# A masked scan over the first tokens of layer 0, with the full scan behind a branch on the chip

## The chip, the cores and the metric

One core of one Trainium2 chip. The metric is the device time of one execution in microseconds (us), as the median of repeated executions. Where two kernels are compared, a ratio is given: the mean time of one kernel's runs over the mean time of the other's runs of the same rounds. It is therefore not quite the ratio of the two medians that are quoted.

The engines in the profile: PE is the matrix engine, PEld its weight loads, DVE the vector engine, ACT the scalar engine, POOL the GpSimd engine, SP the engine that here only issues transfers.

## The reference, cut to what matters

Two layers run one after the other on one picture of 64 x 64 tokens with 96 channels. Each has a group norm, a projection to 192 channels, a 3x3 depthwise convolution, four directional scans with 16 states, a layer norm with a gate, a projection back and a residual add. Layer 1 uses an ordinary recurrence. Layer 0 writes its scan as a quotient and a product:

```python
dt = softplus(dt @ dt_proj_w + dt_proj_b)
A = -exp(A_log)                                     # -1 .. -16 here
log_dA = einsum('bld,dn->bldn', dt, A)
dB_u = einsum('bld,bln->bldn', dt, B_mat) * u[..., None]
decay = exp(cumsum(log_dA, axis=1))                 # over all tokens, never reset
h = decay * cumsum(dB_u / (decay + 1e-12), axis=1)
y = einsum('bldn,bln->bld', h, C_mat) + u * D_skip
```

The decay is the exponential of a sum that only falls. With dt near 0.693, state 1 reaches exp(-110.9) after 160 tokens, and that is exactly 0 in fp32. From there on h is 0 times a finite number, so those tokens add nothing. State n gets there n times sooner. Of 4096 tokens and 16 states, only a small corner has any effect, and the change uses this.

## The kernel before: the parts that the change and the argument touch

The scans work on tiles of 128 rows, 1024 tokens at a time, for two pairs of opposite directions, three tiles and 16 states: 384 iterations in each layer. The parts under `l == 0` are what the change does away with.

```python
def load_exp_ln():
    """Exp, Ln and the copies from one activation table: no reload between them."""
    tc.keep_in_program_order(nc.scalar.preload_act_table_set("natural_log_exp_and_others"))
...
def stage_a(j):                       # one of 384 iterations
    b_ps = broadcast("B", j)          # PE: a selecting product, 2 x 512 columns
    nc.scalar.activation(dec, state[k]["dt"][T], AF.Exp, scale=am[:, T, n : n + 1])
    nc.vector.tensor_mul(b, b_ps, du)
    if l == 0:
        nc.scalar.activation(inv, dec, AF.Ln, bias=eps12)      # 1 / (decay + 1e-12)
        nc.scalar.activation(inv, inv, AF.Exp, scale=-1.0)
        nc.gpsimd.tensor_mul(b, b, inv)
def stage_s(j):
    nc.vector.tensor_tensor_scan(s, dec if l else ones, b, carry..., ALU.mult, ALU.add)
    c_ps = broadcast("C", j)
    if l == 0:
        nc.vector.tensor_mul(dec, c_ps, dec)
        nc.vector.tensor_mul(dec, s, dec)
def stage_r(j):                       # the sum over the states, in PSUM
    nc.tensor.matmul(ps[:, cut], ident, v[:, cut], start=(n == 0), stop=(n == NS - 1))
...
# the close: layer norm, gate, out_proj, residual
for g in range(8):
    nc.tensor.matmul(ps, ipw_s[:, c0 : c0 + m], xn, ...)       # z, fp32, 512 columns
    nc.scalar.activation(sz[b][...], ps, AF.Silu)
load_exp_ln()
for g in range(8):
    nc.tensor.matmul(pc[0], cen, y0[:, cut], start=True, stop=False)   # y minus its mean
    ...
```

## Time and profile before

| | us |
|---|---|
| median of 3 runs | 5496.6 (5489.5 to 5501.2) |
| span of the profiled run | 5493.0 |
| front of layer 0, to the last convolution result | 180.9 |
| scans of layer 0 | 2745.9 |
| gap | 0.2 |
| close of layer 0, to layer 1's first statistics | 136.6 |
| layer 1 | 2429.4 |

The borders of the stages are read from the order of time. The front ends where the last convolution result is copied out, the scans end with the last add into y, and the close starts with PE's next product. Here are only three rows of the costliest groups. Each row gives line, engine, operation, operands and shapes, then how many, then the busy time, the mean of one in ns, and the idle time ahead of them:

```profile
L421 POOL TENSOR_TENSOR b<-b,inv 128x1024 f32<-128x1024 f32 x384 | 1276.9, 3325 | 805.4 <-ACT inv L420 608.5
...
L430 DVE TENSOR_TENSOR_SCAN s<-ones,carry,b 128x1024 f32<-128x1024 f32 x288 | 739.3, 2567 | 1.1 <-POOL b L421 1.1
L430 DVE TENSOR_TENSOR_SCAN s<-dec,carry,b 128x1024 f32<-128x1024 f32 x288 | 688.9, 2420 | 0.0
```

The rows with `ones` are layer 0's scans, those with `dec` are layer 1's. POOL's product with the inverse of the decay is layer 0's alone.

### The profile page before, as it was taken

Reading aid. Unit: us, or ns where it says so; the run is one execution under the profiler, and the core shown is the slowest. Engines: PE = TensorE matmul, PEld = TensorE weight load, DVE = VectorE, ACT = ScalarE, POOL = GpSimd, SP = SyncE. Lnnn points to the kernel's source line nnn. Section 1 sums busy time; section 2 is a strip of 40 time slices with the busy share of each in tenths; the row PEclk is TensorE's granted clock in tenths of the full one; section 3 lists DMA queues with packets and bytes.
Section 4 is the critical chain, followed back from the end, with each engine's and each line's share of the span. In section 5 each row is a group of like instructions: output and inputs, shape, how many; then the busy total and the mean of one; then the engine's idle time right before and its main releaser. Section 6 shows DMA issues by size and latency. Waiting matters only on the chain.

```text
span 5493.0 us, 25105 instructions
## 1 busy us (share of the span) xinstructions
PE 3867.1 (70%) x7592; PEld 1346.8 (25%) x7592; DVE 4677.4 (85%) x3360; ACT 2195.4 (40%) x2729; POOL 2288.8 (42%) x1014
## 2 busy tenths in 40 slices
PE   8766666666666666666677987767676777676678
PEld 2222222222222222222221222222222222222223
DVE  4499999999999999999994429999999999999951
ACT  2355555454454555555553223223232233232221
POOL 0576767666467676676661033123222223121000
PEclk9778778686677777877887568888888888888875
DMA  0000000000000000000000000000000000000000
GB/s 21 0 0 0 0 0 2 0 1 0 0 0 0 0 0 0 0 3 1 0 0 0 0 0 0 0 0 0 0 0 0 0 0 0 0 0 0 0 2 10
DMA packets 11063, 6.67 MB, mean 1 GB/s; under 512 B 10176, under 2 KB 10416, under 8 KB 10928
## 3 DMA queue, kind: packets, MB, share of 16 engines
q1 hardware_dynamic: 8816, 4.30, 0.3%
q8 instruction: 59, 0.97, 0.1%
q10 hardware_dynamic: 2112, 0.79, 0.1%
q14 instruction: 76, 0.62, 0.0%
HBM read 3.51 MB, written 1.57 MB: 1 GB/s over the span
## 4 chain that ended last, share of the span: by engine, by line
DVE 36%; PE 27%; issue 24%; POOL 10%; ACT 2%; DMA 0%; POOLq 0%; DVEq 0%; SPq 0%; ACTq 0%
DVE s L430 17%; PE y L460 11%; DVE b L415 8%; PE cv L251 4%; DVE hc L447 3%; POOL ln L372 3%; DVE dec L443 3%; PE bc_C L401 2%; PE bc_B L401 2%; POOL t L371 2%; DVE dec L442 2%; POOL b L421 1%; POOL du L375 1%; PE in L222 1%; POOL rl L374 1%
## 5 line engine op out<-in xcount | busy, mean ns | idle before, releaser
L421 POOL TENSOR_TENSOR b<-b,inv 128x1024 f32<-128x1024 f32 x384 | 1276.9, 3325 | 805.4 <-ACT inv L420 608.5
L401 PE MATMUL bc_C<-C,sel 96*128 96x512 bf16 x1536 | 553.8, 448 | 1045.0 <-DVE dec L442 536.1
L460 PE MATMUL y<-dec,ident 128*128 128x512 f32 x1536 | 1103.7, 858 | 245.0 <-DVE dec L443 208.1
L413 ACT ACTIVATE dec<-dt,am 128x1024 f32<-128x1024 f32 x768 | 879.7, 1146 | 864.5 <-PE y L460 561.3
L415 DVE TENSOR_TENSOR b<-bc_B,du 128x1024 f32<-128x1024 f32 x768 | 934.3, 1217 | 84.8 <-PE bc_B L401 83.6
L460 PE MATMUL y<-hc,ident 128*128 128x512 f32 x1536 | 921.1, 732 | 21.7 <-DVE uy L473 11.4
L401 PEld LDWEIGHTS <-sel 96*128 96x128 bf16 x3072 | 329.0, 108 | 2175.9 <-issue 2092.4
L430 DVE TENSOR_TENSOR_SCAN s<-ones,carry,b 128x1024 f32<-128x1024 f32 x288 | 739.3, 2567 | 1.1 <-POOL b L421 1.1
L430 DVE TENSOR_TENSOR_SCAN s<-dec,carry,b 128x1024 f32<-128x1024 f32 x288 | 688.9, 2420 | 0.0
L401 PE MATMUL bc_B<-B,sel 96*128 96x512 bf16 x1536 | 529.5, 430 | 124.3 <-DVE b L415 118.3
L439 ACT COPY carry<-s 128x1 f32<-128x1 f32 x576 | 108.4, 188 | 1213.0 <-DVE s L430 1212.4
L460 PEld LDWEIGHTS y<-dec,ident 128*128 128x128 f32 x1536 | 368.7, 264 | 811.2 <-issue 391.2
L443 DVE TENSOR_TENSOR dec<-s,dec 128x1024 f32<-128x1024 f32 x384 | 539.7, 1406 | 0.2
L371 POOL TENSOR_TENSOR t<-w,t 128x512 f32<-128x512 f32 x96 | 138.0, 1438 | 856.1 <-DVE t L370 855.9
L447 DVE TENSOR_TENSOR hc<-bc_C,s 128x1024 f32<-128x1024 f32 x384 | 464.7, 1210 | 1.7 <-PE bc_C L401 1.7
L442 DVE TENSOR_TENSOR dec<-bc_C,dec 128x1024 f32<-128x1024 f32 x384 | 460.9, 1200 | 0.0
L419 ACT ACTIVATE inv<-dec,eps 128x1024 f32<-128x1024 f32 x384 | 440.7, 1148 | 28.0
L460 PEld LDWEIGHTS y<-hc,ident 128*128 128x128 f32 x1536 | 359.4, 236 | 369.7 <-issue 300.9
L420 ACT ACTIVATE inv<-inv 128x1024 f32<-128x1024 f32 x384 | 405.8, 1057 | 11.8
L372 POOL TENSOR_TENSOR ln<-ln,t 128x512 f32<-128x512 f32 x96 | 259.3, 2701 | 7.4
L251 PE MATMUL cv<-pad,diag 64*64 64x512 f32 x288 | 246.3, 1056 | 0.0
L430 DVE TENSOR_TENSOR_SCAN s<-ones,b 128x1024 f32<-128x1024 f32 x96 | 230.2, 2398 | 4.5 <-POOL b L421 4.5
(123 smaller groups left out, 2936.7 us busy)
## 6 DMA issues: line engine op xcount, KB each, us to landing
out_dram<-ob SPq DMA_DIRECT2D x8, 192.0 KB, 2.2
xw<-in_xpw_dram SPq DMA_DIRECT2D x4, 306.0 KB, 2.8
xt<-in_x_dram ACTq DMA_DIRECT2D x4, 192.0 KB, 4.4
xt<-in_x_dram SPq DMA_DIRECT2D x4, 192.0 KB, 3.2
ipw<-in_ipw_dram SPq DMA_DIRECT2D x2, 144.0 KB, 4.3
ab<-in_alb_dram SPq DMA_DIRECT2D x4, 25.5 KB, 3.2
op<-in_opw_dram SPq DMA_DIRECT2D x2, 48.0 KB
dw<-in_dtw_dram SPq DMA_DIRECT2D x4, 18.0 KB
```

The costliest lines, as they stand in the source:

```text
L251: nc.tensor.matmul(ps.rearrange("p (h w) -> p h w", w=HW), diag[:, k, :], pad1[:, r + i : r + i + 8, j : j + HW], start=(k == 0), stop=(k ...
L372: nc.gpsimd.tensor_add(ln, ln, t)
L401: nc.tensor.matmul(ps[:, cut], selector(T, n), state[k][which][:, cut], start=True, stop=True)
L413: nc.scalar.activation(dec, state[k]["dt"][T], AF.Exp, scale=am[:, T, n : n + 1])
L415: nc.vector.tensor_mul(b, b_ps, du)
L419: nc.scalar.activation(inv, dec, AF.Ln, bias=eps12)
L421: nc.gpsimd.tensor_mul(b, b, inv)
L430: nc.vector.tensor_tensor_scan(s, dec if l else ones, b, carry[T][:, n : n + 1] if c else 0.0, ALU.mult, ALU.add,)
L442: nc.vector.tensor_mul(dec, c_ps, dec)
L443: nc.vector.tensor_mul(dec, s, dec)
L447: nc.vector.tensor_mul(hc, c_ps, s)
L460: nc.tensor.matmul(ps[:, cut], ident, v[:, cut], start=(n == 0), stop=(n == NS - 1))
```

## The change: its intent, and the diff

Layer 0 scans 160 tokens for state 1, 80 for state 2, 56 for states 3 and 4, 32 for 5 to 8 and 20 for 9 to 16, for four directions. All are laid end to end in one row of 2560 columns. One masked scan serves many pieces: `state = mask * state + b`, with a mask of 0 at the first token of each piece. The chip then checks that every dropped piece has a decay of exactly 0 (exponent below -105), and only otherwise runs the full scan.

The full scan computed 2 x 3 x 16 x 4096 = 393,216 columns of up to 128 rows. The short one computes 2 x 2560 = 5120 columns, 77 times fewer.

The diff, cut to its core. Comments were also stripped, so the line numbers of the two kernels differ, and the body of the full scan moved into a function unchanged:

```diff
+CUT = ((0, 1, 160), (1, 2, 80), (2, 4, 56), (4, 8, 32), (8, 16, 20))
+GONE = 105.0
 ...
+    def first_tokens(l, pw):
 ...
+            sel4 = po.tile([32, 32, 128], F32, name="sel4")
+            nc.gpsimd.tensor_copy(
+                sel4, ident[0:32, 0:32].unsqueeze(2).to_broadcast([32, 32, 128])
+            )
+            xs = po.tile([128, 2, XS], F32, name="xs")
+            nc.gpsimd.memset(xs, 0.0)
 ...            # six copies of weights into xs; mask memsets; ud = first tokens of u
+            for a, b in ends(u0, ud[0]):
+                nc.vector.tensor_copy(b, a)
 ...            # projection, softplus (Abs, Exp, Ln), running sum s of dt
+                for n0, n1, ln, off in GROUPS:
+                    for n in range(n0, n1):
+                        nc.scalar.activation(de[...], s[:, :, 0:ln], AF.Exp,
+                            scale=am[0:m, T, n : n + 1])
+                    nc.scalar.activation(wi[:, cut], de[:, cut], AF.Ln, bias=eps12[0:m])
+                    nc.scalar.activation(wi[:, cut], wi[:, cut], AF.Exp, scale=-1.0)
+                    nc.gpsimd.tensor_mul(q, q, dt[...])
 ...
+            for ci, (off, wd, parts) in enumerate(CHUNKS):     # 7 chunks
 ...                # PE: B and C of each piece to all rows, by fp32 selecting products
+                for b, m in enumerate((128, 64)):
+                    nc.vector.tensor_mul(bb[:, 0:wd], bp[0:m, 0:wd], w[b][:, cut])
+                    nc.vector.tensor_tensor_scan(
+                        st[:, 0:wd], mask[0:m, cut], bb[:, 0:wd], 0.0, ALU.mult, ALU.add)
+                    nc.vector.tensor_mul(cd[:, 0:wd], cp[0:m, 0:wd], dec[b][:, cut])
+                    nc.vector.tensor_mul(cd[:, 0:wd], cd[:, 0:wd], st[:, 0:wd])
 ...                # PE: the sum over the states, one fp32 product for each state and half
 ...
+            return nc.values_load(flag[0:1, 0:1], min_val=0, max_val=1, ...)
 ...
-        # ---- the four scans ----
 ...
+        if l == 0:
+            bad = first_tokens(l, pw)
+            with tc.If(bad > 0):
+                for g in range(4):
 ...                # y set back to u * D
+                all_tokens(l, pw)
+        else:
+            all_tokens(l, pw)
```

## The prediction

> **What bounds the kernel now.** I read the busy shares by slice first, then a table of stretches, then the order of time at each border, then the groups by shape.
>
> The page's slices (each is 137 us; a digit is tenths busy):
>
> ```profile
> PE   8766666666666666666677987767676777676678
> DVE  4499999999999999999994429999999999999951
> POOL 0576767666467676676661033123222223121000
> ```
>
> DVE shows two plateaus of 9, with a dip between them: the scans of layer 0 and of layer 1. In both, the vector engine sets the pace; POOL is heavy in the first only (it multiplies by 1/decay). The table of stretches (us; busy time and count of PE, weight loads, DVE, ACT, POOL; granted clock) says the same in numbers, one stretch of each kind:
>
> ```profile
> 57.00:181.00 124.00, 123.83 (x145) 32.52 (x144) 26.66 (x23) 20.77 (x25) 0.00 (x0) 1.00 0.00 0
> 1000.00:2000.00 1000.00, 659.52 (x1211) 216.41 (x1209) 955.43 (x626) 526.28 (x577) 632.55 (x239) 0.74 0.00 0
> 3104.00:3228.00 124.00, 123.23 (x146) 31.90 (x145) 25.96 (x23) 21.47 (x26) 0.70 (x1) 0.50 0.00 0
> 3500.00:4500.00 1000.00, 702.98 (x1651) 276.47 (x1651) 930.57 (x649) 295.73 (x438) 238.54 (x155) 0.85 0.00 0
> ```
>
> The convolutions are all PE (124 of 124 us), the scans 93 to 96% DVE. The borders come from the timeline: the last convolution result of layer 0 is copied out at 180.87, layer 0's closing stage starts at 2926.96, and layer 1's statistics at 3063.55:
>
> ```profile
> 180.87 0.68 ACT L259 ACTIVATE uy<-cv,v 64x512 f32<-64x512 f32 x1 [13.93 <-PE cv L251]
> 2926.96 3.94 PE L509 MATMUL z<-xn,ipw 96*128 96x512 f32 x4 [4.82 <-DVE uy L473]
> 3063.55 4.25 DVE L181 BATCH_NORM_STATS2 st<-xT 96x6 f32<-96x512 f32 x7
> ```
>
> So the span of 5493 us is: front of layer 0 181, **scans of layer 0 2746**, its close 137, all of layer 1 2429. Nothing of layer 1 can start early: it reads the finished residual stream.
>
> [...]a load starts at 183.23 and the next copy at 184.52, 1.29 us later. I use 1.28. [...] The trace has both paces: one half of an fp32 product over 512 columns is issued every 0.854 us in the convolution, every 0.427 us in the projections at 187 us. But the profile's own clock column says 1.00 for that slow convolution and 0.50 for layer 1's equally slow one, so I go by durations.
>
> **The change, part by part.**
>
> *Removed:* the stretch from 180.9 to 2927.0, 2746 us, provided the branch skips the full scan. The flag is set only where some channel's sum A*dt over the kept tokens is above -105. Evaluating the reference's own formulas on its inputs, dt lies between 0.6929 and 0.6935 and the weakest of these sums is -110.9; the branch skips.
>
> *Added:* the short scan. Its width is 640+320+448+512+640 = 2560 elements for each of two channel blocks, in 7 chunks. What each engine has to do, with durations by shape from before:
>
> - ACT: the new code lets Exp and Ln alternate without pinning the shared table; the built program's order has 25 table loads between the first token copy and the flag: 25 x 1.283 = 32 us. An activation costs 0.20 us + 0.84 ns per element (629 ns at 512, 1057 at 1024): per block 26 of them over 7680 elements, 11.6 us, two blocks 23; softplus 12 x 0.47 = 6; small copies 5. Sum 66 us, nearly serial.
> - DVE: a multiply is 692 ns at 512 and 1217 at 1024 (0.17 us + 1.03 ns per element), the scan 1.23 and 2.35 us (0.11 + 2.19). A chunk of N in one block is three multiplies and a scan, 0.62 us + 5.28 ns x N: 14 x 0.62 + 5120 x 5.28 ns = 36 us; softplus, cumsum and adds some 17 more.
> - PE: short fp32 products pay their weight load. The closest thing before is layer 1's output product, 96 columns each:
>
> ```profile
> 5400.94 0.74 PE L554 MATMUL o<-op,g 64*128 64x96 f32 x2
> 5401.61 0.50 PEld L555 LDWEIGHTS o<-ident,xT 96*128 96x128 f32 x2 [0.17 <-issue]
> 5401.61 0.74 PE L555 MATMUL o<-ident,xT 96*128 96x96 f32 x2
> 5401.99 0.55 PEld L553 LDWEIGHTS o<-op,g 128*128 128x128 f32 x2
> ```
>
> Three such products repeat every 1.77 us, 0.59 each. The last four chunks have 28 selecting and 56 summing products; half of the latter have 64x64 weights (0.28 us a pair of loads, not 0.50), so about 0.45 each: 84 x 0.45 = 38 us, more than DVE's 22 us for those chunks.
>
> The path in time, from 181: POOL makes the selectors once the convolution's memory is free (4096 elements at 1.04 us per 1024, memsets, six copies) to 188.5; four projection products at the slow pace and their copies to 194; three softplus halves of 4.0 us on ACT (0.47 x 3 + two table loads) to 206; block 0's decays and weights, 10 loads and 13 us of activations, to 232; DVE's cumsum for block 1, 235; first weights of block 1, 242. Only then can the chunks run in their order, block 1 being in each: 33 us of DVE work remain (275), but PE finishes its short products nearer 254 + 38 = 291; I take 286. Copies out of PSUM and twelve adds: 292. **So the new stage is 111 us.** [...]
>
> *Moved:* everything after the branch waits for it. The built order shows layer 0's close now interleaved differently: 10 table loads where there were 2 (Silu between Exp and Ln work), and layer 1's decay constants wait on the scalar queue for weights whose transfers are now issued only after the branch (two of 306 KB, 2.8 us to landing, and four small ones). PE held that stretch (36.0 of 37 us busy), with single PSUM buffers, so ACT's delays show: 8 x 1.28, some under PE's work, plus a few us of DMA: 12 us. Layer 1's matmul order is the same as before, so its 2429 us stay.
>
> Sum: 2746 removed, 111 + 5 + 12 = 128 added, net 2618. 5496.6 - 2618 = 2879; I say **2880**.
>
> **The rivals.** *The branch is taken on the chip:* both scans, about 5620 us. The margin of 5.9 in an exponent and dt's spread of 0.0006 speak against it; 2%. [...] *PE runs warm in the short stage:* its products halve, DVE ends it at 275 to 278, and the time is 2868. For: projections at 187 us ran at 0.427. [...] *The jump stalls:* skipping thousands of instructions on every engine costs tens of us; 2900 to 2920. Nothing before measures it. *Layer 1 changes pace:* its multiplies waited 80 us for broadcasts of PE, so a better or worse granted clock could move it by some 1%; within one trace the clock is steady over each plateau, with no slow drift, which speaks against.
>
> **Range and chances.** Layer 0's front and layer 1 are 2610 us measured and hardly touched; the short stage may be 90 to 150 us, the branch 2 to 25, the close 137 to 165. Unlisted waits between engines add, rarely subtract, so the range leans up: 2840 to 2940. Faster by over 2%: 0.975; within 2%: 0.005; slower: 0.02.
>
> **What would show each step.** Chunk, decay and table-load rows between 181 and about 292, with 25 loads of 1.28 us; no full-scan row of layer 0 at all; PE, not DVE, last in the chunk stage; the gap at the branch under 10 us on every engine; a close of about 149 us; a layer 1 of 2429 us. Wrong would be: a stage far longer than 111 us because hops between engines outweigh the work, or a layer 1 that runs at another pace.

## The result, and the profile after

The changed kernel takes **2870.2 us** (median of 4 runs, 2867.0 to 2875.5) against 5496.5 us for the kernel before (4 runs, 5489.5 to 5501.2). The ratio is 0.522 (0.5215 to 0.523). It gives the right result.

The slices of the page, each now 72 us:

```profile
PE   7966888987676676776676777667767666667888
...
DVE  7125227028999999899999999999999899999221
ACT  1235412133222323232332223233232322222210
POOL 0012000047220322322032223103221301000000
```

Of DVE's two plateaus of 9, only one is left. The short scan lies in the third and fourth slice (143 to 286 us), where DVE has 2 and 5 and ACT 3 and 5: no engine is near full. Of the groups of before, no row of layer 0's full scan is left. Layer 1's row is:

```profile
L336 DVE TENSOR_TENSOR_SCAN s<-dec,carry,b 128x1024 f32<-128x1024 f32 x288 | 688.6, 2419 | 0.0
```

2419 ns against 2420: layer 1 is as it was. The table of stretches of the changed kernel, for the convolution, the short scan and the close (us; busy time and count of PE, weight loads, DVE, ACT, POOL; granted clock, DMA share, GB/s):

```profile
57.00:181.00 124.00, 123.79 (x145) 31.95 (x144) 26.68 (x24) 20.82 (x25) 0.04 (x1) 1.00 0.00 0
180.80:290.70 109.90, 61.73 (x213) 42.08 (x213) 57.62 (x112) 66.86 (x103) 24.24 (x26) 1.00 0.00 1
294.60:438.80 144.20, 124.22 (x157) 27.53 (x158) 36.33 (x66) 41.34 (x59) 0.00 (x0) 0.73 0.01 3
```

The second row is the new stage: in 109.9 us no engine is busy for more than 67. It is a chain through several engines, not the work of one. The granted clock in these rows is no guide: the repeat of this kernel (the first experiment) shows 0.50 for the same convolution, busy for 124.00 of 124 us, where this trace shows 1.00. So PE's pace is read from durations. (The trace lists an fp32 product as two records, its halves: the eight summing products over 128x64 elements are 16 records. The counts of PE are records.) By stage:

| us | before | after |
|---|---|---|
| front of layer 0 | 180.9 | 180.8 |
| scans of layer 0 | 2745.9 | 109.9 |
| gap (branch) | 0.2 | 3.9 |
| close of layer 0 | 136.6 | 144.2 |
| layer 1 | 2429.4 | 2426.3 |
| span | 5493.0 | 2865.1 |

So 2636.0 us went, 3.7 came with the branch, 7.6 with the close, and layer 1 gave 3.1.

Inside the short scan the waits of 181 to 295 us tell the order (who waited for whom: us in total, times, longest):

```profile
POOL fw L521 <- ACT fw L519: 33.5, 8, 5.9
ACT fyt L595 <- PE fy L583: 28.9, 2, 28.6
...
DVE fcd L575 <- PE fy L583: 13.1, 8, 3.4
```

First POOL waits for ACT's weights. Then ACT has long been done and waits for PE's summing products (28.6 us in one piece), and DVE waits for PE too (13.1 us in eight waits), because its buffers come free only when PE has read them. The stretch of the last chunks alone, 247.5 to 288.1 us, shows who holds it:

```profile
247.50:288.10 40.60, 40.58 (x181) 34.51 (x180) 26.03 (x48) 11.54 (x21) 5.08 (x3) 1.00 0.01 1
```

PE is busy for 40.58 of 40.60 us.

The border at the branch, in order of time (start, duration, engine, what, and the idle time before it with its end):

```profile
288.63 2.11 DVE L597 TENSOR_TENSOR uy<-uy,fyt 64x160 f32<-64x160 f32 x6
...
291.31 1.28 ACT L752 ACT_TABLE_LOAD   x1 [2.67 <-ACTq L728]
...
294.61 2.05 PE L761 MATMUL c<-y,cen 128*128 128x512 f32 x2 [6.53 <-DVEq L728]
294.73 1.00 DVE L659 TENSOR_SCALAR xn<-xT,gst 96x512 f32<-96x512 f32 x2 [3.98 <-DVEq L728]
```

DVE ends its last add at 290.74 and does nothing until 294.73. PE waits for DVE's sequencer. That is the gap. What the sequencers do in it is seen by line: L599 loads the flag into a register, L728 is the branch. First the flag's load of DVE, then DVE's and PE's events at the branch (duration in ns as least/median/most, then the start in us):

```profile
L599 DVEq TENSOR_LOAD <-flag x1: 544/544/544, 290.7 to 290.7; - x1
```

```profile
L728 PEldq COMPARE_BRANCH  x1: 3512/3512/3512, 286.8 to 286.8; - x1
...
L728 DVEq COMPARE_BRANCH  x1: 72/72/72, 291.3 to 291.3; - x1
L728 DVEq EVENT_SEMAPHORE  x1: 21/21/21, 294.4 to 294.4; - x1
```

DVE's flag is loaded in 0.54 us and compared in 0.07 us by 291.3, but the next event on DVE is at 294.4. Those 3.1 us lie after the comparison and ahead of the first instruction at the jump's target.

### The profile page after: what moved, and what is told of

It is laid out like the page before. It is cut to its first block, busy times and chain, and to the rows that moved or that the text cites. A ratio compares the mean times of both kernels' runs of the same rounds, so it can differ in the third digit from the quotient of the medians.

```text
span 2865.1 us, 13371 instructions
## 1 busy us (share of the span) xinstructions
PE 2125.8 (74%) x4445; PEld 793.2 (28%) x4445; DVE 2143.1 (75%) x1728; ACT 807.5 (28%) x1189; POOL 498.7 (17%) x356
## 4 chain that ended last, share of the span: by engine, by line
PE 40%; issue 24%; DVE 18%; POOL 5%; ACT 1%; POOLq 0%; DVEq 0%
PE y L366 16%; DVE hc L353 7%; DVE s L336 6%; PE cv L714 4%; PE bc_C L307 4%; PE bc_B L307 3%; DVE b L321 3%; PE z L751 2%; POOL t L277 2%; PE v L771 2%; POOL ln L278 1%; PE in L685 1%; PE c L762 1%; PE c L761 1%; PE c L763 1%
## 5 line engine op out<-in xcount | busy, mean ns | idle before, releaser
L336 DVE TENSOR_TENSOR_SCAN s<-dec,carry,b 128x1024 f32<-128x1024 f32 x288 | 688.6, 2419 | 0.0
L307 PE MATMUL bc_C<-C,sel 96*128 96x512 bf16 x768 | 272.8, 442 | 507.3 <-DVE hc L353 505.9
L321 DVE TENSOR_TENSOR b<-bc_B,du 128x1024 f32<-128x1024 f32 x384 | 467.2, 1217 | 76.4 <-PE bc_B L307 75.5
L319 ACT ACTIVATE dec<-dt,am 128x1024 f32<-128x1024 f32 x384 | 439.1, 1145 | 298.4 <-DVE s L336 297.0
L307 PEld LDWEIGHTS <-sel 96*128 96x128 bf16 x1536 | 159.5, 105 | 959.1 <-issue 907.9
L307 PE MATMUL bc_B<-B,sel 96*128 96x512 bf16 x768 | 247.4, 405 | 3.9 <-DVE b L321 3.2
L336 DVE TENSOR_TENSOR_SCAN s<-dec,b 128x1024 f32<-128x1024 f32 x96 | 227.3, 2394 | 0.0
L278 POOL TENSOR_TENSOR ln<-ln,t 128x512 f32<-128x512 f32 x48 | 114.8, 2391 | 3.8
L714 PEld LDWEIGHTS cv<-pad,diag 64*64 64x64 f32 x288 | 63.9, 223 | 182.2 <-issue 182.2
L230 PE MATMUL pj<-uc,xw 128*96 128x512 f32 (+1 forms) x160 | 88.2, 666 | 23.1 <-DVE rl L271 20.7
L280 POOL TENSOR_TENSOR dt<-ln,rl 128x512 f32<-128x512 f32 x48 | 101.8, 2120 | 3.8
```

What stands on the lines that cost most here:

```text
L230: nc.tensor.matmul(ps[0:m], xw[:, T, c0 : c0 + m], uc[T][:, h * 512 : (h + 1) * 512], start=(T == 0), stop=(T == 2),)
L278: nc.gpsimd.tensor_add(ln, ln, t)
L280: nc.gpsimd.tensor_add(dt, ln, r)
L307: nc.tensor.matmul(ps[:, cut], selector(T, n), state[k][which][:, cut], start=True, stop=True)
L714: nc.tensor.matmul(ps.rearrange("p (h w) -> p h w", w=HW), diag[:, k, :], pad1[:, r + i : r + i + 8, j : j + HW], start=(k == 0), stop=(k ...
```

## The experiments

The theory at the outset had five parts. In the first half of the short stage, ACT's table loads set the pace. In its second half, PE's short fp32 products do. At the branch, DVE's jump over the full scan costs some 4 us. POOL's first work delays the start. In the close, ACT's added table loads cost some 10 us. Its rivals: DVE is the bound of the chunks, the comparison itself (and the flag's load) is what costs at the branch, or the close varies by itself and ACT has nothing to do with it.

The experiments ran in three groups: the first two on one chip, the last (the branch taken, the second early-decay run and the third run of the changed kernel) on another. A first run repeated the changed kernel, as their base.

> The changed kernel once more, as the yardstick of this group: about 2870 us (2866 to 2876), with 110 us from the last convolution result (181) to the last add into y (291), a gap of 4 us at the branch, a close of 144 us and a layer 1 of 2426 us.

Measured: 2877.8 us (2876.2 to 2879.3, 5 runs), ratio 0.523. The profiled run has a short stage of 109.8 us and a close of 148.4 us. The stage is the same to 0.1 us, while the close is 4 us longer. The close of a kernel that did not change already varies, so in the experiments stages are compared by their own borders.

### Tables pinned in the short scan

```diff
+            load_exp_ln()
             sel4 = po.tile([32, 32, 128], F32, name="sel4")
```

> One table that holds Exp and Ln is loaded ahead of the short scan, so 25 loads become 1. My theory (ACT sets the pace until block 1's first weights are there, at 242): 19 of the 25 loads lie before that moment, 19 x 1.283 = 24 us come off, the stage falls from 110 to about 86 us and the time to about 2846 us. Rival 1 (the chunk work of DVE and PE sets the pace throughout): under 5 us. [...]

Measured: 2852.1 us (2825.0 to 2861.2), ratio 0.518 (0.5159 to 0.5203). The stage falls from 109.9 to 92.1 us. ACT's busy time in it falls from 66.9 to 34.4 us, so the loads are gone; 25 x 1.283 = 32.1 us is what they took. Only 17.8 us come off the stage. In the table of stretches, the first row is the whole stage, the second its part from the end of the wait for weights:

```profile
180.40:272.50 92.10, 62.41 (x214) 42.06 (x213) 62.02 (x110) 34.43 (x79) 23.34 (x26) 0.50 0.00 1
...
220.20:270.50 50.30, 48.14 (x193) 37.61 (x192) 35.14 (x62) 9.41 (x25) 6.45 (x5) 0.50 0.00 1
```

From 220 us on PE is busy for 48.1 of 50.3 us, and ACT waits 40.5 us for it in one piece. In the changed kernel this stretch of PE began at 238.5 us and ended at 288.1, so it was as long, and the whole gain lies ahead of it. There stood 19 of the 25 loads, 24.4 us; the other six, 7.7 us, lay beside PE's work and were worth nothing. The loads were the pace of the first half, as the theory said, but its size (24 us, a stage of 86) was not reached: some 18 of the 24.4 us came off, mostly because ACT now waits 5.9 us for DVE ahead of that stretch, against 1.3 before. Rival 1 (under 5 us) is false.

### The sum over the states with bf16 operands

```diff
-                    nc.vector.tensor_mul(cd[:, 0:wd], cd[:, 0:wd], st[:, 0:wd])
+                    cb = wk.tile([m, 512], BF16, tag="cb", name=f"fcb{b}{ci}")
+                    nc.vector.tensor_mul(cb[:, 0:wd], cd[:, 0:wd], st[:, 0:wd])
 ...
-                                    ident[0:m, 0:m],
+                                    idb[0:m, 0:m],        # the identity in bf16
```

The summed terms are rounded to bf16. The outputs are right.

> The products that sum over the states take bfloat16 operands, one pass of TensorE in place of two [...]; DVE's and ACT's instructions stay the same in number and size. Theory (from about 247 on PE's short products, not DVE, set the pace): some 112 half products of the last four chunks become 56, about 10 us less PE work, of which DVE takes back a little: the stage ends 7 to 10 us sooner, 2861 us. Rival (DVE sets the pace of the chunks): under 2 us.

Measured: 2859.7 us (2856.9 to 2865.0), ratio 0.520 (0.5196 to 0.5211). The stage falls to 95.9 us, by 14.0. The stretch of the last chunks in the table:

```profile
247.50:274.00 26.50, 20.27 (x117) 17.01 (x117) 26.40 (x46) 11.59 (x22) 4.44 (x3) 1.00 0.00 2
```

Now DVE is busy for 26.40 of 26.50 us and PE for 20.3. The trace lists one pass in place of two: the summing products over 128x64 elements are 16 records in the changed kernel and 8 here. The theory had the direction, but not the size: PE's work fell by 20.3 us, not by 10, and the stage by 14.0, not by 7 to 10. This is the cleanest reversal: the same chunks, DVE's work unchanged (26.0 us before, 26.4 now), and the bound moved from PE to DVE. The rival "DVE is the bound" is false for the changed kernel. It holds only once PE has been relieved, and 14 us is all that PE held beyond DVE.

### POOL's first work in another order

```diff
-            sel4 = po.tile([32, 32, 128], F32, name="sel4")
-            nc.gpsimd.tensor_copy(sel4, ...)
             xs = po.tile([128, 2, XS], F32, name="xs")
 ...        # xs and mask
+            sel4 = po.tile([32, 32, 128], F32, name="sel4")
+            nc.gpsimd.tensor_copy(sel4, ...)
```

> GpSimd makes the small projection operand first and the selectors (3.66 us) last. Theory (the first projection waits for GpSimd's queue, 6.9 us of PE idle put down to it): projections start 4 to 5 us sooner, the stage is 105 us and the time about 2866 us. Rival (DVE's six token copies, which took 6.7 us beside GpSimd's copy, hold the projection just as long): under 1.5 us.

Measured: 2867.7 us (2839.7 to 2875.1), ratio 0.521 (0.5186 to 0.5229). The time does not separate from the base; the stage does, at 106.2 us, 3.7 less (4 to 5 were expected). The start of the stage in the changed kernel:

```profile
180.93 6.67 DVE L452 COPY ud<-u 128x160 f32<-128x160 f32 x6 [97.17 <-PE cv L714]
180.96 3.66 POOL L414 COPY sel<-ident 32x4096 f32<-32x4096 f32 x1 [156.74 <-PE cv L714]
...
187.73 1.39 PE L460 MATMUL xd<-ud,xs 128*102 128x320 f32 x2 [6.94 <-POOL xs L421]
```

And with the order changed:

```profile
181.14 3.29 DVE L452 COPY ud<-u 128x160 f32<-128x160 f32 x6 [97.17 <-PE cv L714]
...
184.24 1.39 PE L460 MATMUL xd<-ud,xs 128*102 128x320 f32 x2 [3.23 <-POOL xs L417]
```

PE starts 3.7 us sooner after the end of the convolution (it idles 3.23 us, not 6.94). There is a second reading: DVE's six copies took 6.67 us beside POOL's large copy and take 3.29 us without it. In the changed kernel one of the two copies of 128x160 elements took 3.79 us beside POOL's copy of 3.66 us (they ended at 184.7 and 184.6 us), and the other, after them, took 0.38 us. But the copies are not what held PE. In the new order PE starts at 184.24 us, before the last copy ends (184.43), so its first product does not need all six. The two that it needs, of the first two directions, are these copies of 128x160, and in the changed kernel they were done at 185.0 us, 2.7 us before PE began. So POOL's queue was the last wait, as the theory had it.

### Layer 1's decay constants made at the start

In the changed kernel these constants are made after the branch, and their Exp pulls table loads into the close (ten there, of 1.28 us each, against two in this version). This version makes them at the very start:

```diff
+    def decays(l):
 ...        # the load of ab, am = -exp(ab), each with a buffer of its own
+    dec_l = [decays(0), decays(1)]
     for l in range(2):
 ...
-            ab = wts.tile([128, 3, NS + 1], F32, tag="ab", name=f"ab{lp}")
-            nc.sync.dma_start(out=ab, in_=alb[lp])
-            am = wts.tile([128, 3, NS], F32, tag="am", name=f"am{lp}")
-            nc.scalar.activation(am, ab[:, :, 0:NS], AF.Exp)
-            nc.vector.tensor_scalar_mul(am, am, -1.0)
+            ab, am = dec_l[l][p]
```

> Layer 1's decay constants are loaded and made at the very start, so that no Exp of theirs stands among the Silus after the branch; 10 table loads after the branch become 2. Theory (ACT delays PE in the close): the close falls from 144 to about 137 us, as in the kernel before, and the time by 7 us to 2863 us. Rival (PE's slow pace hides it): under 2 us.

Measured: 2854.1 us, ratio 0.5205 (0.5189 to 0.5221). The six runs fall into two groups: 2851.8 to 2855.8 (four) and 2873.8 to 2874.4 (two). The profiled run is of the quick group, with a close of 126.0 us. That looks like 18 to 22 us gained. But the very same kernel was run again later:

> The early-decay variant once more, in the same group as the changed kernel. Same pace on both sides: 0 to 4 us less than the changed kernel (the table loads and the late decay constants cost almost nothing by themselves, since TensorE idled 20 us in the close with 10 loads and with 2). If fewer loads make the quick pace likelier: mostly 2852 here against mostly 2870 beside it.

Measured: 2870.5 us, ratio 0.521 (0.5191 to 0.5228), again in two groups: 2848.6 and 2852.1, and 2870.5 to 2875.4 (three). This time the profiled run is of the slow group. The stretch of the close in the first run:

```profile
295.10:421.10 126.00, 106.05 (x157) 24.52 (x158) 36.24 (x64) 30.83 (x49) 0.00 (x0) 0.78 0.00 0
```

And in the second run of the same kernel:

```profile
294.30:438.80 144.50, 125.05 (x157) 27.49 (x158) 36.24 (x64) 30.81 (x49) 0.00 (x0) 0.67 0.00 2
```

157 records of PE in both, and 30.8 us of ACT in both, without the added loads. PE needs 106 us for them once and 125 us the other time, and it is idle 19.9 and 19.5 us. A row of the groups by shape shows where, in the first run:

```profile
L759 PE MATMUL z<-xn,ipw 96*128 96x512 f32 x16 | 9.8, 697 | 0.0
```

And in the second:

```profile
L759 PE MATMUL z<-xn,ipw 96*128 96x512 f32 x16 | 16.4, 1130 | 0.0
```

The same 16 instructions take 697 ns on average in one run and 1130 ns in the other. The whole difference lies in these first products: all of `z` is done by 316 us in the first run and by 331 us in the second, and the later groups of the close repeat every 13.7 to 13.8 us in both. The close's length is set by PE's pace in that run, and that pace is not of the program alone. The granted clock of the rows (0.78 and 0.67) moves the same way.

### A second branch close by

```diff
                 all_tokens(l, pw)
+            with tc.If(bad > 0):
+                nc.scalar.mul(y0[:, 0:1024], u0[:, 0:1024], ds[:, 0:1])
```

> A second branch on the same flag right behind the first, over one scalar instruction, no second read of the flag. Theory (most of the 4 us is the long jump with a new fetch of instructions, and the meeting of the engines): the second gap is under 1.5 us, 2871 us. Rival (every branch costs the same): a second gap of about 4 us, 2874 us.

Measured: 2857.1 us (2856.1 to 2870.2), ratio 0.5205 (0.5194 to 0.5216), nominally faster by half a per cent although it does more. Its stage is 109.8 us and its gap 4.0 us, against 109.9 and 3.9. A second comparison and a short jump cost about 0.1 us. DVE's events show it: the second comparison takes 56 ns, and the wait of 3.2 us lies between the first comparison (291.3) and its target (294.6), as in the changed kernel:

```profile
L734 DVEq COMPARE_BRANCH  x1: 56/56/56, 294.7 to 294.7; - x1
```

So the gap is not the comparison. What made this version faster is again the close, at 129.3 us:

```profile
294.80:424.10 129.30, 107.95 (x157) 25.45 (x158) 36.33 (x65) 42.17 (x60) 0.00 (x0) 0.76 0.01 3
```

This close has all ten table loads and the same order of ACT's instructions as the changed kernel's, and ACT is even busier (42.2 us against 41.3). It is 15 us shorter, because PE took 108 instead of 124 us. This is the second witness against the theory that ACT's loads make the close long.

### No branch and no fallback

```diff
-            return nc.values_load(flag[0:1, 0:1], ...)
+            return None
 ...
-            bad = first_tokens(l, pw)
-            with tc.If(bad > 0):
-                ...
+            first_tokens(l, pw)
```

It is right for these inputs only: on others, nothing would catch a decay that has not vanished.

> No flag is read, no branch, no fallback (right on these inputs, not safe on others). Theory (the branch costs its own gap and the close has nothing that could have been moved ahead of it): 4 us less, 2866 us. Rival (the branch is a wall to the scheduler): the z products of the close, 31 us of PE, move into the short scan, where PE is idle for most of the first 57 us, and the time falls by 15 to 30 us, to 2840 to 2855 us.

Measured: 2844.8 us (2843.3 to 2850.3), ratio 0.518 (0.5172 to 0.5186), all five runs in the quick group. At the border:

```profile
287.81 1.46 DVE L597 TENSOR_TENSOR y<-y,fyt 128x160 f32<-128x160 f32 x6 [1.22 <-ACT fyt L595]
...
289.37 2.07 PE L750 MATMUL c<-y,cen 128*128 128x512 f32 x2 [0.62 <-ACT fyt L595]
```

PE starts the close's first product 2.1 us before the last add into y has ended. In the changed kernel it starts 3.9 us after that. So the branch costs 3.9 + 2.1 = 6.0 us directly. The rest of the 25 us between the medians is the close, 124.1 us here at the quick pace. The time lies in the rival's range (2840 to 2855 us), but by luck: the close's gate products did not move into the short scan, and the first `z` product starts at 293 us, after the first `c` products. For other work the branch was a wall: without it layer 1's decay constants are made in the short scan (DVE changes a sign for them at 286.2 us), and the close has two table loads, not ten.

### The branch taken

```diff
-GONE = 105.0
+GONE = 1000.0
```

> The threshold is raised to 1000, which no sum reaches, so the flag is set and the full scan runs behind the short one. Theory: the kernel before's 2746 us of layer 0's scans come back on top of everything: 2870 + 2746 + about 8 us for setting y again = 5620 to 5630 us, correct. Rival (the full scan inside the branch is scheduled worse): over 5660 us.

Measured: 5618.8 us (5616.1 and 5621.5), ratio 1.0227. Short scan and full scan run one after the other, as the rival of the prediction had it. The border again:

```profile
288.50 2.04 PE L230 MATMUL pj<-u,xw 128*108 128x512 f32 x2
...
289.37 1.15 ACT L731 ACTIVATE y<-u,ds 128x1024 f32<-128x1024 f32 x1 [0.24 <-DVE y L597]
```

Here nobody jumps over anything. PE goes on without a listed wait, ACT starts 0.24 us after the add that it needs, and POOL starts 0.8 us after DVE's last add (291.25 to 292.01), once DVE has its flag. Flag, load and comparison are the same as in the changed kernel. So of the 4.0 us that DVE stands still there, at most 0.8 is the flag and the comparison, and the other 3.1 to 3.2 us are the **jump over the full scan**. What happens in it the DMA view tells: between 286 and 296 us the changed kernel's trace has six transfers of instructions (8 or 16 KB each). PE, ACT and DVE make their comparisons in this stretch, at 286.8, 288.8 and 291.3 us. Two more lie between 258 and 263 us, around POOL's comparison at 258.9, and only three in the other 101 us from 180 to 286. So the jumps go with a fetch of instructions; how the 3.1 us divide within it is not shown. PE pays for its own jump too (its comparison is on record with 3.5 us, from 286.8 on), but that lies beside work that PE had already been given, and PE waits for DVE in any case.

### The changed kernel a third time, and the parts together

> The changed kernel again, now beside the early-decay variant on one chip. So far its nine timed runs in two groups were all 2867 to 2879 us, while a variant with the same closing code gave 2856 three times of four in another group. If the chip or the session sets TensorE's pace in layer 0's close, most runs here are either all near 2855 or all near 2874, like the variant's beside it. If the code sets it, this kernel stays at 2867 to 2879 and the variant at 2852.

Measured: 2868.8 us (2865.9 to 2877.9), ratio 0.522 (0.5214 to 0.5229). Stage 109.8, gap 4.2, close 148.1, layer 1 2433.6 us. Three profiled runs of the changed kernel have stages within 0.1 us of each other, closes of 144.2, 148.4 and 148.1 us and layers 1 of 2426.3, 2433.6 and 2433.6 us. None of its 14 timed runs is of the quick group.

The last version joins the pinned tables, the bf16 sum, POOL's order and the early decay constants, with branch and fallback kept.

> Pinned table, early decay constants, bfloat16 sums and GpSimd's new order together. If the four gains add: 24 + 7 + 8 + 4.5 = 43 us less, 2827 us, with a stage of about 73 us and a close of 137 us. If the gains lie behind one another (DVE's chunk work of 36 us and softplus take over): 2835 to 2845 us.

Measured: **2818.2 us** (2814.3 to 2841.0), ratio 0.5145 (0.5126 to 0.5165): faster than both kernels, and 2.1% under the 2877.8 us of the changed kernel on the same chip. Part of this is pace: the profiled run has the quick close, 126.1 us. The two slow runs, 2840.5 and 2841.0, are 37 us under the changed kernel, which is what the stage gives. The stage is 72.5 us, 37.4 less:

```profile
180.30:252.80 72.50, 39.82 (x150) 24.62 (x149) 57.66 (x111) 34.34 (x79) 23.52 (x26) 0.50 0.00 1
```

DVE has the largest share now, 57.7 of 72.5 us. Of the four parts three touch this stage; alone they gave 17.8, 14.0 and 3.7 us, 35.5 as a sum, and together they give 37.4. Why the sum is exceeded was not looked into. Its five runs again split: 2814.3 to 2818.2 (three), and 2840.5 to 2841.0 (two).

## Why the prediction was right, point by point

The time, 2870 us, is 10 us under the predicted 2880 and inside the range.

- **What is removed.** Predicted 2746 us. No row of the full scan of layer 0 is left, and the branch skips. Shown, and the taken branch shows the other side: 5619 us, as the rival said (about 5620).
- **The short scan.** Predicted 111 us, measured 109.9, and 109.8 in two repeats. Its steps hold too. There are 25 table loads of 1.28 us. The second block's first weights were predicted for 242 us; POOL starts on them at 241.9 and DVE uses them at 243.5. PE, not DVE, is last: the bf16 version shows it directly. PE's last four chunks were sized at 38 us, and its busy stretch at the end is 40.6.
- **The branch.** The sum of the prediction has 5 us for it, with no trace behind it; the gap is 3.9 to 4.2. The records of the sequencers, the second branch and the taken branch divide the 4.0 us of DVE: 0.6 for flag and comparison, 3.1 for the jump, the rest around them. That instructions are fetched there is seen in the six transfers.
- **Layer 1.** Predicted unchanged at 2429 us; the three runs of the changed kernel show 2426 to 2434.
- **The close: the size was right by luck, the step was wrong.** The prediction put it at 149 us, by adding 12 us for ten table loads, where there were two, and for late weights. It measured 144 to 148; two variants with the same closing code show 129.3 at the quick pace. But the term behind it, "8 x 1.28, some under PE's work, plus a few us of DMA", is not what the runs show. With ten loads and PE at the quick pace the close takes 129.3 us (second branch, and pinned tables). With two loads and the slow pace it takes 144.4 (early constants, again). At the same pace the loads, with the late constants, are worth some 3 us (0 to 4), not 12: 129.3 against 126.0 quick, 144.2 to 148.4 against 144.4 slow. The close of before, 136.6 us, was a mixed case (PE 117 us), so the prediction added its 12 us to a number that need not have held in another run.
- **What was not foreseen at all:** the spread. The prediction wrote of a layer 1 that might change pace by 1% and found none. The pace does change, but in the close, from run to run, by some 20 us. What decides it in a run stays open. It does not follow the table loads, as both counts were seen at both paces. It does not follow the program alone, as one kernel showed both. The traces do show when the pace changes. In the ten profiled runs that skip the full scan by the branch, the half products of `z` first start 0.9 to 1.0 us apart, and from some moment about 0.5 us apart. That moment comes 3.7 to 4.5 us after PE's first product of the close in the four runs with a close of 126.0 to 129.3 us, and 18.6 us or more after it in the six with 143.9 to 148.4 us. What sets the moment is not shown, nor why all 14 timed runs of the changed kernel were slow.
- **The rivals.** "PE runs warm in the short stage", the pace of 0.427 us for a half product, did not come: PE's last chunks held it for 40.6 us, and the repeat shows a clock of 0.50 there. After a table load the next activation starts 0.01 us later (lines below), and taking out the loads took 17.8 us off the stage. "The jump stalls, tens of us" was too much: it stalls, for 3.1 us.

## What to carry to other kernels

A stage that is cut 77-fold in work does not get 77 times shorter (here 25 times), because the work left is small pieces: count table loads, short products and hops between engines, each by a duration from the trace, and follow them in time to see which one ends last. Taking away one limit gives only the distance to the next one: the pinned tables took 32 us off ACT and 18 off the stage. And before an effect of 20 us is put down to a cause, run the same kernel twice and compare the stage's own borders, not the total time.

## What the traces show of single costs

- A table load took 1283 ns in every row of the traces before and after. In the changed kernel's order of time, a load starts 0.02 us after the activation before it and the next activation 0.01 us after the load:

```profile
242.06 1.13 ACT L511 ACTIVATE fdec<-fs,am 64x224 f32<-64x224 f32 x3
243.21 1.28 ACT L518 ACT_TABLE_LOAD   x1
...
244.50 0.67 ACT L518 ACTIVATE fw<-fdec,eps 64x448 f32<-64x448 f32 x1
```

- PE's pace differed between stretches in which it was busy without a gap. In the second early-decay run one goes from 294.3 to 330.3 us, and its last 27 half products of `z` take 26.54 us, 0.98 us each; in the first run 28 of them take 14.48 us, 0.52 each. Layer 0's convolution is busy for 123.8 of 124 us and keeps one pace (144 half products in 123.08 us of the chain before, 0.855 us each). Of eight traces asked for it, five show a clock of 0.50 there and three show 1.00, with 145 or 146 records in all eight, so the profile's clock column can mislead. And a whole stage varies: the same 157 records of PE took 106 us in one run and 125 us in another.
- A compare-and-branch is recorded in the changed kernel with 45 to 72 ns on SP, POOL, ACT and DVE, and with 3512 on PE. The flag's load into a register, 0.46 to 0.54 us per engine, comes on top.
- DVE stood still for 3.1 us after the comparison where it jumped over the full scan. Where the branch was taken, PE went on without a listed wait, and POOL started 0.8 us after DVE's last add.
